# Softmax denominators placed by block transposes and transfers, the mean's tiles read back in exchanged blocks, deeper loads and fewer early mask pieces in a four-layer graph network

## The chip, the cores and the metric

The kernel runs on one core of one Trainium2 chip. The metric is device time in microseconds (us) of one execution; the figure before the change is the median of three runs. The profile is one further execution, recorded by the hardware profiler. TensorE is written PE in profile lines (PEld is its weight load), VectorE DVE, ScalarE ACT, GpSimd POOL and SyncE SP; SP computes nothing and issues transfers (DMAs).

## The reference

A graph network of four layers over 3327 nodes with 512 features and an integer adjacency matrix `adj` of 3327 x 3327. Every layer is followed by a residual and a layer norm. Cut to what matters:

```python
Wh = einsum('ni,hio->hno', h, W)                      # L0: 8 heads of 64
e = leaky_relu(f1[:, :, None] + f2[:, None, :], 0.2)
attention = softmax(where(adj[None] > 0, e, -9e15), axis=-1)
h_prime = einsum('hnm,hmo->hno', attention, Wh)       # L2: the same, then elu
...
keep = (A > 0) & (cumsum(A > 0, axis=1) <= 64)        # L1: first 64 neighbours
nb_mean = keep @ X / maximum(cnt, 1)
xj = leaky_relu(nb_mean @ W_nb.T + b_nb)
xi = leaky_relu(X @ W_line.T + b_line)
return xi + where(cnt > 0, xj, 0)
...
x = layernorm(x + layer(x, adj, ...))                 # L0, L1, L2, L3 in turn
```

L3 is attention as in L2, with 4 heads of 128. Numbers are float32.

## The kernel before

**Tiling.** Nodes are padded to 3328, which is 26 tiles (`NT`) of 128; two halves of 13 tiles (`HALF`, 1664 receiving nodes, `IW`). The transposed adjacency is loaded once as int32 pieces of 128 x 832 (`mask_load`, L547) and turned into an fp8 mask in SBUF (`mask_set`: VectorE L558, or ACT L557). There are 104 pieces: `EARLY` = 82 are handled during L0's projection, the other 22 one per sender tile in the first units of L0's attention, 13 of them on VectorE and 9 on ACT.

**Projection** of a tile: four PE transposes of x (L253), an ACT copy to xT (L255), a reduce (L256), then the matmuls pw (L264), small columns rc, dc and qc on ACT (L265, L268), and VectorE's products vt (L270), which are stored as v. `columns` and `prepare` compute from rc and qc what attention needs for each node (L297 to L315).

**Attention** (`unit`, L357) runs in 8 units for each layer, 2 halves by 4 slots s of 128 features: two heads in a unit for L0 and L2 (`HS` = 2), one for L3. A unit loops over 26 sender tiles j. VectorE makes t from the broadcast row rb, the column qc and the mask (L398, 128 x 1664), ACT makes from t an fp8 step y (L401), PE accumulates po from vj and t in four column cuts (L421) and the denominators pd from y, the mask and pieces of the weights (L373). Then po is copied to ob (ACT L441; in L3's first half VectorE block transposes, L439, and four block transfers to hd, L461), transposed back by PE (pt, L449), copied (hb, L453) and stored to hd by SP (L454). These later steps stand in a list of jobs, one taken for each j of the next unit.

**Denominators.** pd holds for each receiving node partial sums of two kinds in 32-row groups. After a half's last slot (in L3's second half after s=1, 2 and 3) pd is copied to db (ACT L474 and L475, the latter by VectorE in L3), 13 PE matmuls of db with a constant matrix (`sums`, L487) add the parts and put nodes on partitions, and VectorE combines and inverts them (`reciprocals`, L500 to L503). They are the third and fifth job of the next unit, or run directly at a layer's end.

**Finish** (`finish_steps`, L165): for each pair of tiles load h from hd (L126), load xr, divide by the denominators (rec, L180), add or elu (L185 to L194), layer norm (L151 to L161). h and xr have their own buffers.

**sage()** (L610) is layer 1. Stage a: xT (L647, L649), matmuls pz and pi (L655, L658), three bf16 terms of pz, of which one goes to DRAM (zd). Stage b, the mean: for each of 26 tiles 26 x 3 matmuls into acc (L767), with the mask kt made two tiles ahead (PE prefix pk L735, VectorE L739, carries loaded by POOL and copied by ACT L727). `output` (L743) makes the tile's y, normalises it and stores it to x2. The tile's projection for L2 follows as two jobs: `job1` (`project1`) at t = 11 and `job2` (`project2`) at t = 17 of the next tile.

**third()** (L794) normalises L2's output in pairs of tiles and projects them for L3. The loads and steps of one pair are begun before the pair in front of it is projected.

**What sets the order.** PE runs in the order of the program text. On the other engines a scheduler orders the instructions, except where `keep_in_program_order` pins one to its place. Each engine works strictly in its order: an instruction that waits holds up all behind it. SP's transfers, too, are issued in order.

## Time and profile before

| | us |
|---|---|
| median of 3 runs | 3428.16 (3425.46 to 3432.74) |
| profiled execution | 3434.45 |
| its span | 3432.3 |
| PE busy | 3295.2 (96%) |
| VectorE busy | 2666.0 (78%) |
| ACT busy | 2374.3 (69%) |
| mean granted clock of PE | 0.982 |

The span from start to end, by the groups of instructions: L0 projection 0 to 150, L0 attention to 963, sage stage a to 1160, mean 1183 to 1765, L2 attention 1800 to 2572, third 2592 to 2725, L3 attention to 3327 and its tail to 3432; the gaps are changes of stage.

How to read it: "busy" is time in which an engine executes; register, semaphore and transfer-issuing instructions are not counted. A row of instructions has line, engine, operation, output<-input tiles, shapes and count, then busy us and mean ns of one, then the idle time just before it and what ended that. A timeline row has start, length, engine, line, operation and count (neighbouring equal instructions are one row), and in brackets the idle time before it with its releaser. Matmul counts are those of the profile, in which a float32 matmul appears twice.

### The profile page before, as it was taken

The page shows a single profiled execution, that of the slowest core. Times are in us where ns is not written, and L with a number is a line of the kernel's source. Part 1 is how long each engine was busy: PE and PEld are TensorE (multiplying, and loading weights), DVE is VectorE, ACT ScalarE, POOL GpSimd, SP SyncE. Part 2 cuts the span into 40 slices and gives each one's busy share as a digit, 9 for nine tenths or more (in the row PEclk, how much of TensorE's full clock was granted, in tenths as well). Part 3 has the DMA queues.
Part 4 walks back from the last instruction along what each step waited for, and adds up shares of the span by engine and source line. Part 5 has one row for each costly group of instructions (what it writes and reads, how often), then busy time and mean ns, then how long its engine had stood idle before and what let it go on. Part 6 is the DMA issues. An engine that isn't in the chain of part 4 may idle for free.

```text
span 3432.3 us, 47383 instructions
## 1 busy us (share of the span) xinstructions
PE 3295.2 (96%) x18705; PEld 1656.3 (48%) x18705; DVE 2666.0 (78%) x2571; ACT 2374.3 (69%) x2172; POOL 215.1 (6%) x344
## 2 busy tenths in 40 slices
PE   8799999999999899999989999999998999999997
PEld 7544344444444355555543444444446654455553
DVE  5799999999967443434349999999997766668876
ACT  2388999999943233333338999899997655559985
POOL 3200000000010111111110000000001000000000
PEclk9999999999999999999999999999998999999998
DMA  9732111111043422222220111111116411112211
GB/s 372 279 110 69 51 48 43 53 45 39 26 140 125 127 81 76 71 71 73 70 70 25 43 49 48 53 49 46 32 34 219 160 40 40 42 47 89 82 37 48
DMA packets 225061, 276.62 MB, mean 81 GB/s; under 512 B 45949, under 2 KB 160327, under 8 KB 224840
## 3 DMA queue, kind: packets, MB, share of 16 engines
q1 hardware_dynamic: 192280, 162.21, 14.8%
q0 software_dynamic: 27040, 103.70, 9.6%
q10 hardware_dynamic: 5520, 7.69, 0.7%
q8 instruction: 148, 2.42, 0.3%
q14 instruction: 73, 0.60, 0.1%
HBM read 204.92 MB, written 68.60 MB: 80 GB/s over the span
## 4 chain that ended last, share of the span: by engine, by line
PE 73%; issue 12%; DMA 6%; DVE 4%; ACT 3%; POOL 1%; SPq 0%; POOLq 0%; ACTq 0%; DVEq 0%
PE po L421 49%; PE pd L373 7%; PE acc L767 5%; DVE t L398 3%; PE pw L264 3%; PE pz L655 3%; PE pi L658 3%; DMA raw<-in_adjT_dram 2%; DMA cy<-ctd 2%; ACT y L401 1%; PE pt L449 1%; PE pe L487 1%; DMA r<-rr 0%; POOL cy L624 0%; PE pa L966 0%
## 5 line engine op out<-in xcount | busy, mean ns | idle before, releaser
L398 DVE SCALAR_TENSOR_TENSOR t<-rb,qc,mask 128x1664 f32<-128x1664 f32 x1040 | 1959.0, 1945 | 183.1 <-PE po L421 163.6
L401 ACT ACTIVATE y<-t,bi,sc 128x1664 fp8e4<-128x1664 f32 x1040 | 1770.0, 1766 | 321.7 <-PE pd L373 302.9
L421 PE MATMUL po<-t,vj 128*64 128x448 f32 (+3 forms) x8320 | 1912.8, 521 | 24.4 <-DVE t L398 24.2
L421 PEld LDWEIGHTS po<-t,vj 128*64 128x64 f32 (+1 forms) x8320 | 835.0, 148 | 978.1 <-issue 710.6
L767 PE MATMUL acc<-zs,kt 128*128 128x512 bf16 x1352 | 404.7, 381 | 0.0
L767 PEld LDWEIGHTS <-kt 128*128 128x128 fp8e4 x2028 | 199.3, 98 | 246.0 <-issue 9.6
L264 PE MATMUL pw<-wsb,xT 128*128 128x264 f32 (+1 forms) x1248 | 302.7, 398 | 9.6 <-DVE vt L270 5.1
L727 ACT CAST pk<-cy 128x512 f32<-128x512 bf16 x169 | 98.4, 587 | 287.1 <-DVE kt L739 234.0
L264 PEld LDWEIGHTS pw<-wsb,xT 128*128 128x128 f32 x1248 | 241.5, 197 | 55.9 <-ACT xT L255 6.0
L373 PE MATMUL pd<-y,sden 128*32 128x448 fp8e4 (+1 forms) x4160 | 259.4, 342 | 8.2 <-ACT y L401 8.2
L767 PE MATMUL acc<-zl,kt 128*128 128x512 bf16 x676 | 257.5, 381 | 4.6 <-DMA zl<-zd 4.6
L739 DVE SCALAR_TENSOR_TENSOR kt<-pk,mask 128x512 fp8e4<-128x512 f32 x169 | 116.2, 688 | 108.2 <-PE pk L735 107.8
L373 PEld LDWEIGHTS <-sden 128*32 128x32 bf16 x4160 | 117.5, 96 | 160.3 <-issue 137.6
L270 DVE TENSOR_TENSOR vt<-pw,dc 128x256 f32<-128x256 f32 x156 | 59.2, 416 | 136.7 <-ACT dc L265 129.7
L352 POOL DMA_DIRECT2D rb<-r x40 | 21.3, 533 | 1607.9 <-DVE t L398 1593.4
L268 ACT COPY rc<-pw 128x8 f32<-128x8 f32 (+1 forms) x78 | 12.7, 163 | 151.0 <-PE pw L264 151.0
L655 PE MATMUL pz<-wn,xT 128*128 128x512 f32 x208 | 93.7, 593 | 1.2 <-ACT xT L649 1.2
L658 PE MATMUL pi<-wl,xT 128*128 128x512 f32 x208 | 93.5, 592 | 0.0
L558 DVE TENSOR_SCALAR mask<-raw 128x832 fp8e4<-128x832 int32 (+2 forms) x95 | 56.2, 600 | 45.6 <-DMA raw<-in_adjT_dram 45.2
L747 DVE SCALAR_TENSOR_TENSOR y<-acc,cnt,bnb 128x512 f32<-128x512 f32 x26 | 19.5, 751 | 88.5 <-PE acc L767 88.5
L624 POOL DMA_DIRECT2D cy<-ctd x91 | 67.9, 746 | 289.5 <-ACT pk L727 264.8
L256 DVE TENSOR_REDUCE xsum<-xT 128x4 f32<-128x512 f32 x78 | 53.0, 681 | 39.7 <-ACT xT L255 39.3
(175 smaller groups left out, 1738.4 us busy)
## 6 DMA issues: line engine op xcount, KB each, us to landing
vj<-v SPq DMA_DIRECT2D x312, 128.0 KB
rb<-r POOLq DMA_DIRECT2D x40, 832.0 KB, 4.6
raw<-in_adjT_dram SPq DMA_DIRECT2D x67, 416.0 KB
cy<-ctd POOLq DMA_DIRECT2D x78, 256.0 KB, 3.9
h<-hd SPq DMA_DIRECT2D x61, 256.0 KB
v<-vt SPq DMA_DIRECT2D x50, 256.0 KB
hd<-hb SPq DMA_DIRECT2D x48, 256.0 KB
xr<-x POOLq DMA_DIRECT2D x45, 256.0 KB, 3.1
```

What stands on the lines that cost most here:

```text
L264: nc.tensor.matmul(pw[e][:, :FW + H], xT[:, c, :], wsb[:, c, e, :], start=c == 0, stop=c == FC - 1)
L270: nc.vector.tensor_tensor(vt[:, hs, :], pw[e][:, :FW].rearrange("p (h d) -> p h d", d=D), self.dc[:, t, hs].rearrange("p (h e) -> p h e", e=1)
L373: nc.tensor.matmul(pd[c][32 * kk:32 * kk + 32, :w_], lhsT, rhs, start=(kk, c) not in seen, skip_group_check=final is not None, stop=last a ...
L398: nc.vector.scalar_tensor_tensor(t, rb[k], self.qc[:, j, h:h + 1], mask[:, j, i0:i0 + IW], op0=ALU.max, op1=ALU.mult)
L401: nc.scalar.activation(y, t, AF.Sigmoid, bias=self.bi[:, j, h:h + 1], scale=self.sc[:, j, h:h + 1], saturate=False)
L421: nc.tensor.matmul(po[c][k * D:(k + 1) * D, :z - a_], vj[:, j % 2, k * D:(k + 1) * D], ts[k][:, a_:z], start=j == 0, stop=j == NT - 1)
L624: nc.gpsimd.dma_start(out=cy[:, :n, :], in_=ctd[t:t + n, b * GW:(b + 1) * GW] .rearrange("(o t) i -> o t i", o=1).to_broadcast([P, n, GW]))
L655: nc.tensor.matmul(pz, xT[:, c, :], wn[:, c, :], start=c == 0, stop=c == FC - 1)
L658: nc.tensor.matmul(pi, xT[:, c, :], wl[:, c, :], start=c == 0, stop=c == FC - 1)
L727: nc.scalar.copy(pks[k % 2], carry[b, t // 4 * 4][:, t % 4:t % 4 + 2, :])
L739: nc.vector.scalar_tensor_tensor(kt, pk, NEIGHBOURS, mask[:, t:t + 2, i0:i0 + GW], op0=ALU.is_le, op1=ALU.mult, saturate=False)
L767: nc.tensor.matmul(acc, kts[t][:, s * P:(s + 1) * P], zs(t, c) if c < 2 else zl[:, t, :], start=t == 0 and c == 0, stop=t == NT - 1 and c ...
```

## The change

It has four parts. In all but the last of the denominator steps, `sums` and the db copies give way to VectorE's 32 x 32 block transposes of pd, two reduces over the three elements of each sum, four small transfers to a DRAM buffer dd and one transfer back as pes, with nodes on partitions; `finish_sums` then does what `reciprocals` did, as the seventh job of the next unit, at the end of a layer as the last job (in L3's s=2 after five empty jobs). In the mean, tiles 0 to 24 are read back from x2 by four transfers with 32 x 32 blocks exchanged, so that a block transpose on VectorE, pinned in the program's order, gives xT; `job1` comes at t = 17 of the next tile and `job2` at t = 11 of the one after. In third() loads are begun three pairs ahead, with 10 h and 6 xr buffers, the first pairs' h on POOL. `EARLY` is 68, so that 36 pieces fall into attention: 22 on VectorE, 14 on ACT.

In the order built, SP has 100 issues for yx and 35 for dd and pes more than before; on PE 25 x 4 transposes and 7 x 13 matmuls are gone. At half time of L0 and L2 `finish_sums` begins nine tiles of t behind the reduces, in L3 8, 3 and 3.

```diff
@@ -162,7 +162,7 @@
-    def finish_steps(pool, xin, layer, t0, n, hbufs=6, eng=nc.sync):
+    def finish_steps(pool, xin, layer, t0, n, hbufs=6, eng=nc.sync, xbufs=None):
         H, D = layer.H, layer.D
         ys, xs, steps = [], [], []
@@ -171,7 +171,7 @@
                 h = pool.tile([P, F], F32, name="h", bufs=hbufs)
                 load_tile(h, hd, t, eng)
                 ys.append(h)
-                xr = pool.tile([P, F], F32, name="xr")
+                xr = pool.tile([P, F], F32, name="xr", bufs=xbufs)
                 load_tile(xr, xin, t, nc.gpsimd)
                 xs.append(xr)
@@ -247,12 +247,16 @@
             nc.gpsimd.memset(self.sm, 0.0)
-        def project1(self, pool, ps, xt, t):
-            pt = ps.tile([P, FC, P], F32, name="pt")
-            for c in range(FC):
-                nc.tensor.transpose(pt[:, c, :], xt[:, c * P:(c + 1) * P], ident)
+        def project1(self, pool, ps, xt, t, blocks=False):
             xT = pool.tile([P, FC, P], F32, name="xT")
-            nc.scalar.copy(xT, pt)
+            if blocks:
+
+                tc.keep_in_program_order(nc.vector.transpose(xT, xt))
+            else:
+                pt = ps.tile([P, FC, P], F32, name="pt")
+                for c in range(FC):
+                    nc.tensor.transpose(pt[:, c, :], xt[:, c * P:(c + 1) * P], ident)
+                nc.scalar.copy(xT, pt)
             nc.vector.tensor_reduce(xsum[:, :, t], xT, AX.X, ALU.add)
             return xT
@@ -467,48 +471,79 @@
             if s < NS - 1 and not (final and s > 0):
                 return jobs
+
+            ss = slice(0, NS) if not final else slice(0, 2) if s == 1 else slice(s, s + 1)
+            hs = slice(ss.start * HS, ss.stop * HS)
+            r_ = rec[:, t0:t0 + HALF, :H].rearrange("p t (s k) -> p t k s", k=HS)
+            rc = self.rc[:, t0:t0 + HALF, :].rearrange("p t (s k) -> p t k s", k=HS)
             db = sp.tile([P, WA], F32, name="db", bufs=1)
             if WB < WA:
                 nc.gpsimd.memset(db[64:, WB:], 0.0)
+            if not (final and s == NS - 1):
+
+
+                for c in range(2):
+                    nc.vector.transpose(db[:64, c * (WA // 2):(c + 1) * (WA // 2)], pd[c][:64, :WA // 2])
+                    nc.vector.transpose(db[64:, c * (WB // 2):(c + 1) * (WB // 2)], pd[c][64:, :WB // 2])
+                red = sp.tile([P, WA // 32, 2, NS], F32, name="red", bufs=1)
+                dv = db.rearrange("p (b s x) -> p b s x", s=NS, x=8)
+                for o in range(2):
+                    nc.vector.tensor_reduce(red[:, :, o, :], dv[:, :, :, 3 * o:3 * o + 3], AX.X, ALU.add)
+                dd = dram.tile([IW, 2, 2 * NS], F32, name=f"dd{self.li}{half}{s}")
+                for kk in range(4):
+                    i_, w_ = (0, WA) if kk < 2 else (WA, WB)
+                    nc.sync.dma_start(out=dd[i_:i_ + w_, kk % 2, :].rearrange("(b i) x -> i b x", i=32),
+                                      in_=red[32 * kk:32 * kk + 32, :w_ // 32].rearrange("p b o s -> p b (o s)"))
+                pes = sp.tile([P, HALF, 2, 2, NS], F32, name="pes", tag="red", bufs=1)
+                nc.sync.dma_start(out=pes.rearrange("p q k o s -> p q (k o s)"),
+                                  in_=dd.rearrange("(q p) k x -> p q (k x)", p=P))
+
+                def finish_sums():
+                    if HS == 1:
+
+                        tc.keep_in_program_order(
+                            nc.vector.tensor_tensor(pes[:, :, 0], pes[:, :, 0], pes[:, :, 1], op=ALU.add))
+                    for k in range(HS):
+                        ins = nc.vector.scalar_tensor_tensor(r_[:, :, k, ss], pes[:, :, k, 0, ss], 2.0, rc[:, :, k, ss],
+                                                             op0=ALU.mult, op1=ALU.mult)
+                        if HS > 1:
+                            tc.keep_in_program_order(ins)
+                        nc.vector.scalar_tensor_tensor(r_[:, :, k, ss], pes[:, :, k, 1, ss], -2.0, r_[:, :, k, ss],
+                                                       op0=ALU.mult, op1=ALU.add)
+                    nc.vector.reciprocal(rec[:, t0:t0 + HALF, hs], rec[:, t0:t0 + HALF, hs])
+
+                jobs += [nothing] * max(0, 6 - len(jobs))
+                at = 6 if half == 0 or s < NS - 1 else len(jobs)
+                if final and s > 1:
+
+                    return [nothing] * 5 + [finish_sums] + jobs[2:]
+                return jobs[:at] + [finish_sums] + jobs[at:]
+
             for c in range(2):
                 nc.scalar.copy(db[:64, c * (WA // 2):(c + 1) * (WA // 2)], pd[c][:64, :WA // 2])
-                (nc.scalar.copy if HS == 2 else nc.vector.tensor_copy)(
-                    db[64:, c * (WB // 2):(c + 1) * (WB // 2)], pd[c][64:, :WB // 2])
+                nc.vector.tensor_copy(db[64:, c * (WB // 2):(c + 1) * (WB // 2)], pd[c][64:, :WB // 2])
             held = []
             def sums():
-                pe = po[0][:, :2 * HALF * H].rearrange("p (q o h) -> p q o h", q=HALF, o=2) if final and s == NS - 1 else \
-                    qp.tile([P, HALF, 2, H], F32, name="pe", tag="q")
+                pe = po[0][:, :2 * HALF * H].rearrange("p (q o h) -> p q o h", q=HALF, o=2)
                 held.append(pe)
                 for q in range(HALF):
                     e = int(q >= NA)
-                    cc = c1[:, :, 8 * e:8 * e + 8] if HS == 2 else c1w[:, :, e, :]
-                    nc.tensor.matmul(pe[:, q, :, :], db[:, (q - e * NA) * P:(q - e * NA + 1) * P], cc,
+                    nc.tensor.matmul(pe[:, q, :, :], db[:, (q - e * NA) * P:(q - e * NA + 1) * P], c1w[:, :, e, :],
                                      start=True, stop=True)
-
             def reciprocals():
                 pe = held[0]
-
-                ss = slice(0, NS) if not final else slice(0, 2) if s == 1 else slice(s, s + 1)
-                r_ = rec[:, t0:t0 + HALF, :H].rearrange("p t (s k) -> p t k s", k=HS)
-                rc = self.rc[:, t0:t0 + HALF, :].rearrange("p t (s k) -> p t k s", k=HS)
-                pv = pe.rearrange("p t o (k s) -> p t o k s", k=HS)
-                for k in range(HS):
-                    tc.keep_in_program_order(
-                        nc.vector.tensor_tensor(r_[:, :, k, ss], pv[:, :, 0, k, ss], rc[:, :, k, ss], op=ALU.mult))
-                    nc.vector.tensor_tensor(r_[:, :, k, ss], pv[:, :, 1, k, ss], r_[:, :, k, ss], op=ALU.add)
-                hs = slice(ss.start * HS, ss.stop * HS)
+                nc.vector.tensor_tensor(r_[:, :, 0, ss], pe[:, :, 0, ss], rc[:, :, 0, ss], op=ALU.mult)
+                nc.vector.tensor_tensor(r_[:, :, 0, ss], pe[:, :, 1, ss], r_[:, :, 0, ss], op=ALU.add)
                 nc.vector.reciprocal(rec[:, t0:t0 + HALF, hs], rec[:, t0:t0 + HALF, hs])
-            if final and s == NS - 1:
-
-                take = []
-                return [lambda: take.append(transposed(*QUADS[0])), lambda: take.append(transposed(*QUADS[1])),
-                        sums, reciprocals] + [lambda q=q: take[q]() for q in range(2)] + \
-                    [lambda q=q: transposed(*q)() for q in QUADS[2:]]
-            return jobs[:2] + [sums, nothing, reciprocals] + jobs[2:]
+
+            take = []
+            return [lambda: take.append(transposed(*QUADS[0])), lambda: take.append(transposed(*QUADS[1])),
+                    sums, reciprocals] + [lambda q=q: take[q]() for q in range(2)] + \
+                [lambda q=q: transposed(*q)() for q in QUADS[2:]]
@@ -749,7 +784,14 @@
                     nc.vector.scalar_tensor_tensor(y, y, cnt[:, 2, t:t + 1], xi, op0=ALU.mult, op1=ALU.add)
                     norm_rows(sp, [y], t)
                     store_tile(dst, y, t, nc.sync)
-                    return y
+                    if t == NT - 1:
+                        return y
+
+                    yx = sp.tile([P, FC, P], F32, name="yx")
+                    for q in range(4):
+                        nc.sync.dma_start(out=yx[32 * q:32 * q + 32].rearrange("p c (g f) -> p c g f", g=4),
+                                          in_=dst[t * P:(t + 1) * P, :].rearrange("(g a) (c q f) -> q a c g f", g=4, q=4, f=32)[q])
+                    return yx
                 carry_in(0)
                 kts = kept(0, 0) + kept(0, 2)
@@ -771,13 +813,13 @@
                                              len(ahead) < min(NT, t + 10) and t % 2 == 1):
                                 ahead += kept(b + 1, len(ahead))
-                            if jobs and (t == 11 or t == 17 and not (last and s == G - 1)):
+                            if jobs and (t == 11 and t0 + s > 1 or t == 17):
                                 jobs.pop(0)()
                         y = output(acc, t0 + s)
                         held = {}
                         def job1(y=y, t=t0 + s, held=held):
-                            held["xT"] = nxt.project1(sp, ps, y, t)
+                            held["xT"] = nxt.project1(sp, ps, y, t, t < NT - 1)
                         def job2(t=t0 + s, held=held):
                             nxt.project2(sp, bank, wsb, held["xT"], t)
@@ -807,11 +849,25 @@
                 def bank(e):
                     return ps.tile([P, 512], F32, name=f"pw{e}")
+
                 pend = None
                 ahead = first
+                groups = []
+
+                def load_group(t0):
+                    if t0 < NT:
+                        groups.append(finish_steps(fp, x2, L2, t0, 2, 10, nc.gpsimd if t0 < 4 else nc.sync, 6))
+                        groups[-1][1].pop(0)()
+
+                for t0 in (2, 4):
+                    load_group(t0)
                 for t0 in range(0, NT, 2):
-                    ys, ahead = ahead, finish(fp, x2, L2, t0 + 2, 2, 6, nc.sync if t0 else nc.gpsimd) \
-                        if t0 + 2 < NT else None
+                    ys = ahead
+                    load_group(t0 + 6)
+                    if groups:
+                        ahead, steps = groups.pop(0)
+                        for f in steps:
+                            f()
                     for s, y in enumerate(ys):
                         t = t0 + s
                         store_tile(x3, y, t, nc.sync)
@@ -945,7 +1001,7 @@
                 nc.gpsimd.memset(mask[:, NT - 1, :], 0.0)
             nc.gpsimd.memset(mask[:, :, N:NP], 0.0)
             pieces = [(t, q) for t in range(NT) for q in range(2)] + [(t, q) for q in (2, 3) for t in range(NT)]
-            EARLY = 3 * NT + 4
+            EARLY = 5 * NT // 2 + 3
             msteps = mask_steps(rw0, pieces[:EARLY], 5, (), False, 8)
             def load(t):
```

## The prediction

> **What bounds the kernel now.** I read the busy digits first, then the busy time of each engine stage by stage, since the bound changes with the stage. Columns: stretch and its length, then busy time (instructions) of PE, PEld, DVE, ACT and POOL, granted clock, DMA share, GB/s.
>
> ```profile
> 150.00:963.00 813.00, 790.40 (x5819) 338.41 (x5819) 804.26 (x490) 742.41 (x500) 12.13 (x24) 0.99 0.18 54
> 963.00:1160.00 197.00, 192.20 (x543) 94.39 (x544) 130.49 (x248) 69.56 (x120) 14.69 (x27) 0.97 0.38 125
> 1183.00:1765.00 582.00, 569.96 (x2658) 296.50 (x2656) 228.05 (x421) 205.66 (x364) 78.87 (x113) 0.99 0.26 77
> 1800.00:2572.00 772.00, 764.35 (x5458) 344.81 (x5456) 768.97 (x436) 720.13 (x478) 9.62 (x16) 0.99 0.13 41
> 2592.00:2725.00 133.00, 118.63 (x556) 98.78 (x557) 99.88 (x239) 97.64 (x203) 11.82 (x22) 0.95 0.59 193
> 2725.00:3327.00 602.00, 599.07 (x2524) 304.75 (x2522) 429.36 (x349) 412.71 (x294) 17.08 (x30) 1.00 0.21 58
> ```
>
> These are attention of L0, sage stage a, the mean (stage b), attention of L2, third(), attention of L3. In L0 and L2 VectorE is busy 99% and sets the pace; TensorE, at 97%, follows it. In the mean and in L3 TensorE is the bound and VectorE has 60% and 29% free. So VectorE work added in L0 and L2 costs its full time, added in the mean or L3 nothing; TensorE work saved counts only in the mean and L3, and at the starts of stages, where the chain goes from engine to engine.
>
> **Fewer mask pieces first.** 14 pieces (82 to 68) leave the L0 projection. The last 14 mask sets on VectorE there stand at 131.75 to 149.2, mixed with the value products (L270), and wait for their loads; the first t of attention starts at 149.69. Without them the last L270 follow ACT's dc (143.1), and L311 to L315 (1.5 us) end near 145.1: -4.5 (-3.5 if something else there is late, -5 at best). In attention 22 instead of 13 pieces fall to VectorE, 14 instead of 9 to ACT. Nine sets at 0.59 us (L558, 587 ns here) on a full VectorE: +5.3; the five on ACT (0.97 us each) lie in its 9% of room. Sum +0.8.
>
> **Denominators.** Removed: seven of eight groups of 13 matmuls (L487), and ACT's db copies. Added on VectorE for each: four block transposes, two reduces; on SP five small transfers. Rows for the prices:
>
> ```profile
> L256 DVE TENSOR_REDUCE xsum<-xT 128x4 f32<-128x512 f32 x78 | 53.0, 681 | 39.7 <-ACT xT L255 39.3
> ...
> L439 DVE STREAM_TRANSPOSE ob<-po 128x448 f32<-128x448 f32 x8 | 4.7, 625 | 0.0
> ...
> L439 DVE STREAM_TRANSPOSE ob<-po 128x384 f32<-128x384 f32 x8 | 4.0, 541 | 0.0
> ```
>
> Transposes 2 x 0.62 + 2 x 0.54 = 2.3 (64 lanes take as long as 128: the 64x384 copy took 0.557). A reduce of 336 elements a lane lies between the 256-element product's 0.416 and 0.681: 0.5, two are 1.0. The four scalings and the reciprocal cost what they did (4 x 0.21 + 0.80). In L0 and L2 at half time this lands on the bound: 3.3, less the 0.44 that VectorE idles there now (577.58): +2.9 each, **+5.8**. TensorE's 3 us saved there buy nothing. Lower end +2, if ACT's freed 2 us help; upper +9, if the results come late (below).
>
> In L3 TensorE is the bound, and three groups go (half time, s=1, s=2; the last one stays). One displaces 2.82:
>
> ```profile
> 3063.80 2.96 PE L487 MATMUL pe<-c1w,db 128*128 128x8 f32 x26
> 3066.62 4.74 PE L421 MATMUL po<-t,vj 128*128 128x448 f32 x8
> ```
>
> 3 x 2.82 = **-8.5** (-6 to -9.5). VectorE's new work is covered by its room; its finishing step stands behind 3 to 8 tiles of t, 8.7 to 23 us, and three t buffers (8.7 us of PE) cover a stall.
>
> The round trip is the unknown: four transfers in 32-byte rows (3328), then one in 64-byte rows (1664), which SP issues only when the four have landed. Nearest row: L3's block transfers hd<-ob, 128-byte rows, four issues, 6656 packets. DMA busy share in 40 slices of 0.55 us:
>
> ```profile
> DMA  0000016299999479999951000000053000000000
> ...
> hd<-ob SPq DMA_DIRECT2D x4, 208.0 KB
> ```
>
> From 2811.4 fifteen slices, 8.3 us: 1.25 ns a row. A 256 KB load (xi, 2.9 us to landing; 0.7 of it bytes at the 365 GB/s that L0's projection reaches) leaves 2.2 us fixed. By rows: 4.15 + 2.2, then 2.1 + 2.2 = 10.6 us. By bytes (106 KB each, at that row's 100 GB/s): 2 x (1.1 + 2.2) = 6.6 us. I take 10.6: that row is the nearest, and it moves small pieces. At half time nine tiles of t (16.8 us at 1.86) hide it. At the two layer ends nothing does. End of L0:
>
> ```profile
> 962.91 0.84 PE L487 MATMUL pe<-c,db 128*128 128x16 f32 x6 [1.97 <-ACT db L475]
> 965.48 4.45 PE L487 MATMUL pe<-c,db 128*128 128x16 f32 x20 [1.72 <-ACT db L475]
> ...
> 972.97 1.75 PE L647 MATMUL pt<-ident,h 128*128 128x128 f32 x8
> ...
> 984.85 0.66 PE L647 MATMUL pt<-ident,h 128*128 128x128 f32 x4 [1.84 <-ACT h L161]
> ```
>
> Without the sums tile 0's transposes (972.97) come about 7 us earlier. But tile 2's (984.85) need its norm, which on VectorE stands behind the first scaling, and that now waits for pes. pd ends at 960.9; transposes and reduces to 964.7; 10.6 more is 975.5; 7.6 of VectorE (scalings, L180, L194, L152 of tiles 2 to 4 in the order built) and 1.2 of ACT follow: 984.3. So the 7 us turn into idle before tile 2: **-1** (by bytes -4.5, and -8.5 if nothing waited). End of L2, alike: tile 0's transposes move from 2592.09 to about 2586.5 (tile 2's h is now loaded behind the weights on POOL, and L180 for it stands before tile 0's rs on VectorE), but pes lands near 2592, tile 2's transposes near 2598.8 against 2600.58, with the clock cold again after that idle: **-1** (-6 to +2).
>
> **Mean: read-back in place of transposes.** 25 of 26 tiles lose four PE transposes and an ACT copy; VectorE gets a 128x512 transpose (0.7, covered). Price on the bound, from the last matmul before to the next after:
>
> ```profile
> 1511.70 0.38 PE L767 MATMUL acc<-zl,kt 128*128 128x512 bf16 x1
> 1512.93 0.66 PE L253 MATMUL pt<-ident,y 128*128 128x128 f32 x4 [0.85 <-ACT y L161]
> 1513.43 0.59 PE L767 MATMUL acc<-zs,kt 128*128 128x512 bf16 x2
> ```
>
> Matmuls start 0.216 apart, so this gap costs 1.5; untroubled ones cost 0.44. Over the 25: **-16.5** (-11 if the waits for y only move elsewhere).
>
> The transpose is pinned on VectorE and waits for y's store and four read-backs; queued behind it are the next tile's y chain and kt. y's chain takes 9.2 us from the last acc (1503.70 to the store at 1512.90). Read-back X: store 2.9, 2048 rows at 1.25 ns 2.6, landing 2.2: near 8. Chain and read-back form a loop of 9.2 + X against the tile's 22.3 (22.98 measured, less 0.67): X may be 13. The Trainium skill ("VectorE: DVE Perf Modes", section "The three transpose paths") warns here: a plain DMA whose access pattern does the transposing is 19 times slower than the hardware's own path when the innermost stride is large. By that, 0.7 us of bytes become 13 (an estimate), X about 18, and the mean loses 25 x 5. The row stands against it: hd<-ob also exchanges blocks, keeps 128 bytes together, and moves 832 KB in 8.3 us, 3.6 times slower than 365 GB/s, not 19. I go by the row.
>
> **Deeper loads in third().** TensorE waits for ACT's h (L161) at 2627.39, 2646.81 and twice later: 9.7 us, plus 1.4 of cold clock (5.02 for 3.67). Under them VectorE waits 5.2 for xr and 5.7 for h. Loads three pairs ahead end these waits, not the table loads (1.28 each) in the same chain: **-6** (-3 to -10).
>
> **Sum.** 0.8 + 5.8 - 8.5 - 1 - 1 - 16.5 - 6 = -26.4. The profiled execution took 3434.45 (span 3432.3, 2.15 around it); it becomes 3408. It lies 6.3 above the median of 3428.16; I take the difference off the median: **3402**.
>
> **Rivals.** (1) The round trip is short or hidden: the ends give -8.5 and -6.7, third -9, the rest as above: -42, 3387. For it: packets themselves are short. Against: two fixed costs in series at each end. (2) VectorE pays more: finishing steps wait in L0 and L2 (+9), the ends give 0 and +2, the mean only -11, third -3: 0.8 + 9 + 2 - 11 - 3 - 8.5 = -11, 3417. For it: SP issues transfers in order behind vj loads. (3) Slower than before: the read-back loop takes over. It decides from X = 13, and eats the whole change at 13 + 26.4/25 = 14.1; at the skill's 18 the time is 3402 + 125 = 3527. Only the row against it makes it unlikely. (4) The change does nothing: the built order shows the matmuls and transposes gone, so no.
>
> **Chances.** Forecast 0.52, (1) 0.28, (2) 0.17, (3) 0.03, (4) 0. The forecast's unknowns reach from 3391 to 3411; the range 3380 to 3417 takes in (1) and most of (2). A measurement tells 0.2% (6.9 us) from no change: faster 0.92, same 0.05 (the far part of (2), the near part of (3)), slower 0.03.
>
> **What would show it.** Right: mean stage near 566; units of L0 and L2 at half time near 100 instead of 97.7; L3 shorter by 8; VectorE's scaling waiting for pes at both layer ends, and TensorE idle before tile 2. Wrong: no wait for pes there (then the ends give 15), the pinned transpose waiting so long that the acc matmuls stall, or idle before kt.

## The result and the profile after

| | before | after |
|---|---|---|
| median, us | 3429.25 (3425.46 to 3432.74, 4 runs) | 3408.52 (3406.53 to 3410.87, 4 runs) |
| ratio | | 0.994 (0.9923 to 0.9957) |
| profiled execution | 3434.45 | 3407.9 |
| its span | 3432.3 | 3406.2 |

I cut both spans at the same events: the first t of L0's attention, the last pd of L0, the first pk of the mean, the first t and last pd of L2, the first po of L3, the end. Stage lengths in us, with some experiments beside them:

| kernel | to first t | L0 attention | sage a | mean | L2 | third | L3 | span |
|---|---|---|---|---|---|---|---|---|
| before | 149.69 | 811.25 | 206.17 | 620.34 | 788.25 | 147.08 | 709.52 | 3432.3 |
| after | 142.95 | 817.71 | 211.35 | 600.76 | 789.98 | 143.18 | 700.27 | 3406.2 |
| difference | -6.7 | +6.5 | +5.2 | -19.6 | +1.7 | -3.9 | -9.3 | -26.1 |
| late_pt | 141.88 | 818.80 | 212.27 | 612.00 | 789.96 | 144.31 | 699.58 | 3418.8 |
| mid_pe | 141.44 | 814.68 | 209.69 | 603.76 | 786.56 | 140.09 | 701.08 | 3397.3 |
| early82 | 146.09 | 815.29 | 211.08 | 600.88 | 789.99 | 141.89 | 699.18 | 3404.4 |
| l3_pe | 141.49 | 817.82 | 210.59 | 603.58 | 790.02 | 140.76 | 713.04 | 3417.3 |
| best_b | 142.42 | 814.76 | 206.73 | 603.39 | 786.62 | 139.20 | 698.78 | 3391.9 |

These are profiled executions. By the medians the change saves 20.7 us: the profiled execution of before was itself 5.2 above its median (3434.45 for 3429.25), which flatters the -26.1.

Where the code of a stage is the same, it differs between the runs by 0.1 us in L2 (apart from yx3, 0.5, and yx2, 2.1), 1.3 in L0's attention, 2.5 in L3, 3.2 at the start and in sage a, and 4.3 in third; a difference is read against that.

Busy time by stretch of after (columns as in the table before):

```profile
143.00:961.00 818.00, 794.99 (x5796) 344.29 (x5797) 812.48 (x504) 743.83 (x498) 10.37 (x19) 0.99 0.20 61
1183.00:1754.00 571.00, 562.94 (x2585) 288.21 (x2584) 243.42 (x447) 191.34 (x339) 79.64 (x114) 0.99 0.35 93
2563.00:2706.00 143.00, 117.22 (x563) 98.39 (x561) 111.85 (x268) 102.67 (x208) 17.68 (x33) 0.92 0.65 215
2706.00:3307.00 601.00, 598.07 (x2476) 300.36 (x2475) 438.52 (x368) 411.08 (x294) 17.28 (x31) 1.00 0.22 59
```

The bounds are the old ones: VectorE fills L0 (99%), TensorE the mean and L3 (99%). What is new is the DMA share of the mean, 0.35 for 0.26; third() is still the stretch of these with most room on TensorE (82% busy).

**Half time of L0** answers to the unit where TensorE had 26 matmuls pe. VectorE, then SP:

```profile
568.42 0.64 DVE L486 STREAM_TRANSPOSE db<-pd 64x448 f32<-64x448 f32 x1
569.08 0.59 DVE L487 STREAM_TRANSPOSE db<-pd 64x384 f32<-64x384 f32 x1
...
572.82 0.98 DVE L491 TENSOR_REDUCE red<-db 128x112 f32<-128x336 f32 x2
...
590.48 0.21 DVE L507 SCALAR_TENSOR_TENSOR rec<-pes,rc 128x52 f32<-128x52 f32 x1
```

```profile
573.83 2.08 SPq L495 DMA_DIRECT2D dd<-red  x4
...
577.66 0.38 SPq L498 DMA_DIRECT2D pes<-dd  x1
```

The transposes, 2 x (0.64 + 0.59), and the reduces, 0.98, cost 3.4; the prediction had 3.3. SP needs 4.2 us from the first issue to the last, and pes is used 12.8 us after it was issued, without a wait. From its first t to that of the next unit the unit took 101.54 us, for 98.62 before: 2.9 more. In L2 it took 101.37 for 99.67, only 1.7 more, because before lost time there in another way: around its matmuls pe TensorE was granted a clock of 0.83, and VectorE was busy for 18.47 of 20 us, where after had 1.00 and 20.00 (before first, then after; the clock is the third number from the right):

```profile
2190.00:2210.00 20.00, 20.00 (x128) 9.87 (x126) 18.47 (x16) 15.33 (x10) 0.20 (x1) 0.83 0.05 14
2190.00:2210.00 20.00, 19.96 (x140) 9.09 (x136) 20.00 (x17) 18.63 (x14) 0.00 (x0) 1.00 0.14 40
```

**End of L0.** SP, VectorE, TensorE and ACT of after, one block each:

```profile
962.18 0.98 SPq L458 DMA_DIRECT2D hd<-hb  x2
964.19 10.69 SPq L495 DMA_DIRECT2D dd<-red  x4
974.98 1.02 SPq L458 DMA_DIRECT2D hd<-hb  x2
977.25 0.36 SPq L498 DMA_DIRECT2D pes<-dd  x1
```

```profile
963.21 0.96 DVE L491 TENSOR_REDUCE red<-db 128x112 f32<-128x336 f32 x2
979.80 0.22 DVE L507 SCALAR_TENSOR_TENSOR rec<-pes,rc 128x52 f32<-128x52 f32 x1 [15.63 <-DMA pes<-dd]
```

```profile
964.19 1.36 PE L682 MATMUL pt<-ident,h 128*128 128x128 f32 x8 [1.17 <-ACT h L161]
975.61 6.38 PE L690 MATMUL pz<-wn,xT 128*128 128x512 f32 x8 [10.06 <-ACT xT L684]
981.83 3.60 PE L693 MATMUL pi<-wl,xT 128*128 128x512 f32 x8
988.31 1.11 PE L682 MATMUL pt<-ident,h 128*128 128x128 f32 x4 [2.89 <-ACT h L161]
```

```profile
974.30 0.77 ACT L457 COPY hb<-pt 128x512 f32<-128x512 f32 x2 [9.45 <-DMA hd<-hb]
974.98 1.07 ACT L684 COPY xT<-pt 128x512 f32<-128x512 f32 x2
```

ACT and SP of before at the same place:

```profile
974.42 0.90 ACT L453 COPY hb<-pt 128x512 f32<-128x512 f32 x2 [1.78 <-DMA hd<-hb]
975.23 1.07 ACT L649 COPY xT<-pt 128x512 f32<-128x512 f32 x2
```

```profile
971.50 3.89 SPq L454 DMA_DIRECT2D hd<-hb  x3
```

The same four issues that took 2.08 us at half time take 10.69 here. VectorE waits 15.63 for pes. A second wait was not foreseen. hb has two buffers. Without the sums in front of them, its first two stores are issued at 962.18 instead of from 971.50, ahead of dd in SP's order, but into the traffic of the stage's loads. The third copy into hb waits 9.45 for the first of these stores, until 974.30, 12.1 us after its issue; in before that copy comes at 974.42, 2.9 us after the store's issue. Behind the copy stands xT, for which TensorE idles 10.06, so that tile 0's pz starts at 975.61, no earlier than in before (975.87). Tile 0's transposes come 3.5 us after pd's end (before: 12.0), but tile 2's 27.7 us after it (before: 23.9).

**Mean.** Where TensorE had four transposes (pt) for each tile, after has none for tiles 0 to 24. VectorE, from kt to the next y, and SP's issues for the same tile:

```profile
1440.08 0.69 DVE L774 SCALAR_TENSOR_TENSOR kt<-pk,mask 128x512 fp8e4<-128x512 f32 x1 [0.42 <-PE pk L770]
1441.33 0.71 DVE L254 STREAM_TRANSPOSE xT<-yx 128x512 f32<-128x512 f32 x1 [0.56 <-DMA yx<-x]
1442.08 0.69 DVE L260 TENSOR_REDUCE xsum<-xT 128x4 f32<-128x512 f32 x1
1446.56 0.75 DVE L782 SCALAR_TENSOR_TENSOR y<-acc,cnt,bnb 128x512 f32<-128x512 f32 x1 [3.79 <-PE acc L809]
```

```profile
1433.81 0.33 SPq L133 DMA_DIRECT2D x<-y  x1
1436.92 2.61 SPq L792 DMA_DIRECT2D yx<-x  x4
```

From the store of y to the transpose pass 7.5 us, of which VectorE waits 0.56; all its waits for yx in the mean are 11.4 us in 11 cases, none over 1.8, and in these 11 tiles the way from store to transpose takes 7.5 to 9.1 us. In most others it is 10.3, without a wait for yx: there VectorE's order, not the read-back, sets the time of the transpose. VectorE then still waits 3.79 for acc: TensorE stays the bound. Tiles follow each other after 22.12 and 21.47 us in turn, where it was 22.9 and 21.9.

**L3, half time.** The row that answers to pe between po and po is a row without a gap:

```profile
3039.70 10.21 PE L425 MATMUL po<-t,vj 128*128 128x448 f32 x29
```

**third().** TensorE's waits for h in the whole stage (total, times, longest), from 2575.7 to 2723 in before and from 2562.7 to 2706 in after, and then the rows in after where they fall at its start:

```profile
PE pt L253 <- ACT h L161: 13.6, 5, 3.9
```

```profile
PE pt L258 <- ACT h L161: 10.6, 3, 8.8
```

```profile
2575.44 1.97 PE L258 MATMUL pt<-ident,h 128*128 128x128 f32 x8 [10.61 <-DMA xr<-x]
2577.28 4.34 PE L268 MATMUL pw<-wsb,xT 128*128 128x260 f32 x16
2590.47 1.12 PE L258 MATMUL pt<-ident,h 128*128 128x128 f32 x4 [8.85 <-ACT h L161]
```

The wait of 10.61 for tile 0 is put down to xr; tile 0 still comes 12.7 after pd's end, for 16.4 in before. In before 3.9 of the 13.6 is the wait for tile 0 (2592.09), and tile 2 (2600.58) doesn't wait at all; the other four waits make 9.7. Of these later waits 1.7 is left in after. But tile 2 now waits 8.85, so that the stage is only 3.9 shorter.

### The profile page after: what moved, and what is told of

The parts are those of the page before. It is cut to its first block, busy times and chain, and to the rows that moved or that the text cites. A ratio compares the mean times of both kernels' runs of the same rounds, so it can differ in the third digit from the quotient of the medians.

```text
span 3406.2 us, 47019 instructions
## 1 busy us (share of the span) xinstructions
PE 3262.8 (96%) x18423; PEld 1631.0 (48%) x18423; DVE 2695.3 (79%) x2630; ACT 2351.4 (69%) x2128; POOL 214.7 (6%) x344
## 4 chain that ended last, share of the span: by engine, by line
PE 79%; issue 7%; DVE 6%; DMA 4%; ACT 2%; POOL 0%; SPq 0%; ACTq 0%; POOLq 0%; DVEq 0%
PE po L425 49%; PE acc L809 9%; PE pd L377 7%; PE pw L268 5%; DVE t L402 4%; PE pz L690 3%; PE pi L693 3%; DMA raw<-in_adjT_dram 2%; ACT y L405 1%; PE pt L453 1%; DMA cy<-ctd 1%; PE pk L770 1%; PE pt L258 0%; PE pa L1022 0%; DVE mask L593 0%
## 5 line engine op out<-in xcount | busy, mean ns | idle before, releaser
L425 PE MATMUL po<-t,vj 128*64 128x448 f32 (+3 forms) x8320 | 1924.6, 520 | 25.0 <-DVE t L402 22.3
L425 PEld LDWEIGHTS po<-t,vj 128*64 128x64 f32 (+1 forms) x8320 | 848.3, 148 | 978.2 <-issue 689.7
L356 POOL DMA_DIRECT2D rb<-r x40 | 21.9, 548 | 1617.0 <-DVE t L402 1604.5
L272 ACT COPY rc<-pw 128x8 f32<-128x8 f32 (+1 forms) x78 | 12.7, 163 | 138.7 <-PE pw L268 136.2
L782 DVE SCALAR_TENSOR_TENSOR y<-acc,cnt,bnb 128x512 f32<-128x512 f32 x26 | 19.5, 751 | 85.9 <-PE acc L809 85.9
```

Source lines behind the costliest of these rows:

```text
L425: nc.tensor.matmul(po[c][k * D:(k + 1) * D, :z - a_], vj[:, j % 2, k * D:(k + 1) * D], ts[k][:, a_:z], start=j == 0, stop=j == NT - 1)
```

## The experiments

The theory: the parts act as the prediction has them, and at the layer ends the round trip is lengthened by loads that share the transfers. The rivals: the round trip is slow by itself, from its short rows, whatever runs beside it; the mean gained only from the later place of the jobs, not from the transposes; and the read-back is near the length at which its loop would slow the mean. Each kernel changes the kernel after in one place, unless said otherwise. The kernel before was timed again beside them: 3431.66 us beside ends_pe, no_wl, late_pt and one_pair, 3432.43 beside mid_pe, early82, ramp2 and best_a2, 3431.24 beside the rest.

**ends_pe** and **mid_pe**: the denominators of L0 and L2 by TensorE again, in the first at the layers' ends, in the second at half time. **l3_pe**: the same for L3's three groups.

```diff
-            if not (final and s == NS - 1):
+            if not (final and s == NS - 1) and not (HS == 2 and half == 1):   # ends_pe
+            if not (final and s == NS - 1) and not (HS == 2 and half == 0):   # mid_pe
+            if not (final and s == NS - 1) and not (HS == 1):                 # l3_pe
```

(The db copies, `sums` with c1, `reciprocals` and `return jobs[:2] + [sums, nothing, reciprocals] + jobs[2:]` of before are put back for these.)

> The changed kernel, but the denominators at the ends of L0 and L2 are summed by TensorE again, as before the change; the half-time and L3 denominators stay with VectorE and the transfers. Theory (the dd and pes round trip sits on the path at the two layer ends, because its small rows share the DMA engines with the next stage's loads, and SP's stores and ACT's copies queue behind it): from the end of L0's pd to the first pk of the mean 206 us again instead of 211.4 (-5.2), from the end of L2's pd to L3's first po 139 to 141 instead of 143.3 (-2 to -4): about 3401 us. Rival (the time at the ends is lost to the shifted loads, masks or clock, not to the round trip): both stretches stay within 1 us of the changed kernel's, about 3408 us.

> The changed kernel, but at half time of L0 and L2 the denominators are summed by TensorE again, as before the change; layer ends and L3 stay with VectorE and the transfers. Theory (VectorE sets the pace there, so its 3.4 us of transposes and reduces cost about their time): L0's attention takes 814.7 us instead of 817.7, L2's 788.3 instead of 790.0, in all 4 to 5 us less, ratio to before 0.9926. Rival (TensorE's saved matmuls and ACT's saved copies pay for it): no difference of more than 1 us in either.

> The changed kernel, but L3's denominators are summed by TensorE again, as before the change; L0 and L2 stay with VectorE and the transfers. Theory (TensorE is the bound in L3 and three groups of 13 matmuls displace 2.8 us each): from L3's first po to the end 708.5 to 710 us instead of 700.3, about 8.5 to 9 us slower than the changed kernel, ratio to before 0.996 to 0.997. Rival (VectorE's new steps and the pes wait in L3 cost what the matmuls save): within 2 us of 700.3.

ends_pe: 3406.59, ratio 0.9924 (0.9909 to 0.9939). Sage a is 207.01 for 211.35, so transposing at L0's end loses 4.3 us. The other profiles bear it out: the four kernels with TensorE's sums there (before, ends_pe, best_a2, best_b) have 206.2 to 207.0, the nine with the round trip and wl's load 209.1 to 212.3. At L2's end TensorE's sums gain nothing: tile 2 comes 29.4 after pd's end, 27.7 in after, so that the theory came true at the first end only. mid_pe: 3401.15, 0.9908 (0.9893 to 0.9923); L0's attention is 3.0 and L2 3.4 shorter than in after, the price of VectorE's work on its own bound. l3_pe: 3419.22, 0.9966 (0.9953 to 0.9979); L3 is 12.8 longer than in after. Its half time:

```profile
3039.69 5.75 PE L425 MATMUL po<-t,vj 128*128 128x448 f32 x16
3045.28 3.34 PE L536 MATMUL pe<-c1w,db 128*128 128x8 f32 x26
3048.47 5.89 PE L425 MATMUL po<-t,vj 128*128 128x448 f32 x8
```

Three times 3.19 (3045.28 to 3048.47) is 9.6. The other 3.2 us lie in the clock: in this stretch l3_pe was granted 0.83 and after 1.00, which over 20 us is 3.4 (an estimate from these two rows, l3_pe first). l3_pe's L3 is also 3.5 longer than before's (709.52).

```profile
3036.00:3056.00 20.00, 20.00 (x92) 11.58 (x93) 12.44 (x13) 8.26 (x7) 0.20 (x1) 0.83 0.37 63
3036.00:3056.00 20.00, 20.00 (x85) 10.37 (x84) 17.67 (x17) 10.43 (x6) 0.20 (x1) 1.00 0.44 68
```

**no_wl**: the 1 MB load of wl at L0's end is left out and pi uses wn (so pi is computed from the wrong weights).

```diff
-                wl = load_w(wp, wlT, "wl", nc.gpsimd)
+                wl = wn
```

> The changed kernel without the 1 MB load of wl: pi is computed with wn instead, so xi has the wrong weights; nothing else is left out. Theory (contention with the stage's loads stretches the dd transfers at the end of L0): SP's four dd issues there take 3 to 8 us instead of 10.7, and pes is there 13 us or less after the reduces instead of 15.6. Rival (32-byte rows cost the same wherever they run): dd issues stay at 10 to 11 us and VectorE's wait at 15 to 16 us.

3401.7 in one run. SP and VectorE:

```profile
965.72 5.85 SPq L495 DMA_DIRECT2D dd<-red  x4
```

```profile
975.69 0.69 DVE L180 TENSOR_TENSOR h<-h,rec 128x512 f32<-128x512 f32 x1 [5.34 <-DMA h<-hd]
976.86 0.21 DVE L507 SCALAR_TENSOR_TENSOR rec<-pes,rc 128x52 f32<-128x52 f32 x1 [0.48 <-DMA pes<-dd]
```

The issues take 5.85 for 10.69, and from the first of them to that of pes pass 8.5 us (965.72 to 974.23) for 13.1; at half time it was 3.8. So wl's load makes up about half of what the round trip loses here; the stage's other loads stayed, and what they cost alone wasn't tried. Tile 2 comes 20.0 after pd's end for 27.7, but not all of that is the load's price. pes is used 11.1 us after dd's first issue for 15.6, which is 4.5. The other 3.2 come from VectorE's order, which is another one in this kernel: three steps L180 stand in front of the first scaling with pes instead of behind it, and from that scaling to tile 2's transposes it takes 5.3 us for 8.5. The wait for pes itself (0.48) is short because VectorE waits 5.34 for an h just before it.

**one_pair** (third()'s loop as before) and **ramp2** (only one pair is loaded ahead of the loop, and ahead of the weights wsb; the next follow later, and from the fifth tile on the loads are as deep as in after):

```diff
-                    ys = ahead
-                    load_group(t0 + 6)
...
+                    ys, ahead = ahead, finish(fp, x2, L2, t0 + 2, 2, 6, nc.sync if t0 else nc.gpsimd) \
+                        if t0 + 2 < NT else None
```

```diff
-                for t0 in (2, 4):
-                    load_group(t0)
+                due = list(range(2, NT, 2))
+                load_group(due.pop(0))
+                wsb = wp.tile([P, FC, 2, FW + L3.H], F32, name="wsb")
...
-                    load_group(t0 + 6)
+                    while due and due[0] <= (2, 6)[t0 // 2] if t0 < 4 else due and due[0] <= t0 + 6:
+                        load_group(due.pop(0))
```

> The changed kernel with third() loading one pair ahead as before the change. Theory (deeper loads remove the later waits for ACT's h, 6 to 7 us, while the start is ruled by the round trip of the denominators): from the end of L2's pd to L3's first po 149 to 151 us instead of 143.3, TensorE waiting for ACT h some 9 us more after tile 4: about 3415 us. Rival (the deeper loads themselves crowd the dd transfers at the start, and give back what they gain): the four dd issues fall from 8.1 to under 5 us, and the stretch stays within 2 us of 143.3.

> The changed kernel with the loads of third() growing from one pair ahead at its start to three pairs ahead from the fifth tile on, and the first pair's loads issued before the weights'. Theory (the deeper loads gain later and cost at the start, where they and the weights come before tile 2's h and share the DMA engines with dd): tile 2's transposes come 22 to 24 us after L2's last pd instead of 27.7, four dd issues under 7 us, and from there to L3's first po 136 to 140 us instead of 143.2. Rival (the later waits do not depend on depth, so the start is only moved): 142 to 144 us.

one_pair: 3413.28, 0.9946 (0.9932 to 0.9961); third 143.59. Its SP issues:

```profile
2571.22 4.40 SPq L495 DMA_DIRECT2D dd<-red  x4
```

against, in after:

```profile
2568.35 8.12 SPq L495 DMA_DIRECT2D dd<-red  x4
```

and VectorE's wait for pes is 0.27 for 5.85. I split third() at tile 2's transposes:

| us | pd's end to tile 2 | tile 2 to L3 |
|---|---|---|
| before | 24.9 | 122.2 |
| one_pair | 22.8 | 120.8 |
| after's third(), eight kernels | 27.1 to 28.2 | 112.5 to 116.6 |
| ends_pe (after's third(), sums on TensorE) | 29.4 | 114.1 |
| best_b (ramp2's third(), sums on TensorE) | 26.8 | 112.4 |

So the rival came true: the deeper loads gain 4 to 8 us once the stage runs and lose 4.3 to 5.4 at its start. The loss is there with TensorE's sums too (29.4 in ends_pe for 24.9 in before, 4.5), so it isn't the round trip alone: with either way of summing, tile 2 comes later when more is loaded ahead. In one_pair TensorE's later waits for h are as short as in after (2.0 from 2592 to 2725), but 5.2 for vt and 5.2 for rr stand in their place, in after 2.2 and 1.6; why was not tried. ramp2: 3403.52, 0.9916 (0.9901 to 0.9931), third 140.33; dd's issues take 10.13 and tile 2 comes at 27.2. The start wasn't cured, against the theory, and the gain isn't beyond the 4.3 by which this stage scatters.

**late_pt**: no read-back, TensorE transposes as before, but the jobs at after's later places.

```diff
-                    yx = sp.tile([P, FC, P], F32, name="yx")
...
-                    return yx
+                    return y
...
-                            held["xT"] = nxt.project1(sp, ps, y, t, t < NT - 1)
+                            held["xT"] = nxt.project1(sp, ps, y, t)
```

> The changed kernel with the new places of the two projection jobs in the mean (t = 17, and t = 11 of the tile after) but with TensorE's four transposes and ACT's copy in place of the read-back. Theory (11 us of the mean's gain are TensorE time, the rest, 6 to 9 us, are waits for y that the later place alone removes): the stretch from the first pk to L2's first t takes 611 to 613 us against 600.8 with the read-back and 620.4 before: about 3419 us. Rival (the later place is what gains): the stretch stays under 604 us, about 3409 us. Second rival (the whole gain is the transposes'): 619 to 621 us, about 3427 us.

3417.45, 0.996 (0.9946 to 0.9975). The mean takes 612.00: of its 19.6 us, 8.3 come from the later places alone (before to late_pt) and 11.2 from the transposes, 0.45 for each of 25 tiles. In late_pt the transposes stand between other matmuls without a wait for y:

```profile
1446.59 0.38 PE L802 MATMUL acc<-zl,kt 128*128 128x512 bf16 x1
1446.81 0.60 PE L258 MATMUL pt<-ident,y 128*128 128x128 f32 x4
1447.24 0.59 PE L802 MATMUL acc<-zs,kt 128*128 128x512 bf16 x2
```

In before such waits make 2.4 us in seven tiles (1205 to 1755), and 2.0 of the 8.3 lie behind the last tile; where the rest lies is open.

**early82**: `EARLY = 3 * NT + 4`, as before.

> The changed kernel with 82 mask pieces in L0's projection again, as before the change. Theory by the profiles (14 pieces fewer bring the first t forward by 6.8 us, and the pieces moved to attention cost 3.6 us there): first t at 149 to 150 us instead of 143, L0's attention 814 us instead of 817.7, about 3 us slower in all. Rival, the prediction's own sum (-4.5 and +5.3): 0.8 us faster in all.

3406.75, 0.9926 (0.9911 to 0.9941). The first t is 1.5 to 4.7 later than in the three kernels beside it, L0's attention 2.4 shorter than in after: nothing in sum that these runs can tell from zero.

**yx2**, **yx3**: the four read-backs twice and three times over, `for q in [0, 1, 2, 3] * 2` and `* 3`. This tests the rival whose loop was to decide from X = 13.

> The changed kernel, but every read-back of the mean is made twice, one after the other into the same tile. Theory (chain of y and read-back form a loop of 9 + X, X is 8 us in the changed kernel and one more pass costs 4 to 5, so the loop takes 21 to 22 us against a tile's 21.8): the stretch from the first pk to L2's first t takes 601 to 612 us instead of 600.8. Rival (the read-back is no loop, VectorE's room hides any length): 601 us here and also with three passes. Second rival (any lengthening is paid at once): 25 x 4.5, over 700 us.

> The changed kernel, but every read-back of the mean is made three times, one after the other into the same tile. Theory (loop of 9 + X with X near 17, so 26 against a tile's 21.8): tiles about 4 us apart more than in the changed kernel, the stretch from the first pk to L2's first t 690 to 720 us, about 3510 us in all. Rival (no loop): 601 to 605 us.

One run each: 3421.74 and 3423.62; the mean takes 615.35 and 617.40. VectorE and SP of yx3:

```profile
1404.26 0.75 DVE L782 SCALAR_TENSOR_TENSOR y<-acc,cnt,bnb 128x512 f32<-128x512 f32 x1 [5.78 <-PE acc L809]
...
1411.38 0.69 DVE L774 SCALAR_TENSOR_TENSOR kt<-pk,mask 128x512 fp8e4<-128x512 f32 x1 [1.38 <-PE pk L770]
1411.99 0.70 DVE L254 STREAM_TRANSPOSE xT<-yx 128x512 f32<-128x512 f32 x1
```

```profile
1391.00 0.33 SPq L133 DMA_DIRECT2D x<-y  x1
1393.54 12.58 SPq L792 DMA_DIRECT2D yx<-x  x12
```

X, the time from store to transpose, is 21.0 (1391.00 to 1411.99), and the loop formula asks for 30 us a tile. Tiles follow after 21.9 and 22.3, so that neither theory came true. The transpose now stands behind the next tile's y (L782), not ahead of it as in after: the pin doesn't hold y's chain back, and the scheduler took the chain first. In yx2 X is about 16.4, with the same order in 23 of 25 tiles. What the longer read-back costs in yx3 is 0.2 to 0.4 us in most tiles, a wait of 7.0 on the last read-back's transpose at the end of the stage, where after waits 3.9, and a longer tile where L2's preparation falls (33.93 for 26.88). The loop of the prediction exists only in the order of after, and no run has a long X in that order: what it would cost there was not measured.

**best_a2** and **best_b**: ramp2's third(), and TensorE's sums again in L0 and L2; best_a2 keeps the transposes at L2's end (`not (HS == 2 and not (self.li == 2 and half == 1))`), best_b nowhere in L0 and L2 (`not (HS == 2)`).

> The changed kernel with TensorE's sums at half time of L0 and L2 and at the end of L0, the round trip kept at the end of L2 and in L3, and the growing loads of third() of the run before. Theory: L0's attention 814.7 us, end of L0 to the mean 207, L2's attention 788.3, third 136 to 140, the rest as in the changed kernel: 11 to 15 us faster than it, ratio to before about 0.990. Rival (each saving only exposes the next wait): less than 7 us faster than it.

> The changed kernel with TensorE's sums in all of L0 and L2, half time and ends, the round trip only in L3, and the growing loads of third(). Theory (every round trip that stands on a path or on a full VectorE is gone): like the run best_a2 (3397.2 us span) but for the start of third, where the sums stand before the transposes again but no pes is waited for: 3394 to 3399 us. Rival (the end of L2 is better with the round trip): 3400 us or more.

best_a2: 3397.61, 0.99 (0.9884 to 0.9917). best_b: 3394.38, 0.9893 (0.9877 to 0.991), the fastest, its interval clear of after's, though not of best_a2's. It keeps what pays where TensorE is the bound (mean, L3), and gives back 3.0 in L0's attention, 4.6 in sage a and 3.4 in L2. Its mean, like that of the other kernels with TensorE's sums in part, is 2.6 to 4.1 longer than after's. The tile with the preparation takes 28.46 for 26.88, and behind it, from 1480 to 1520, all five were granted a clock of 0.96 and after 1.00, which over 40 us is that 1.6 (an estimate); the rest, and what lowers the clock, was not tried.

## Why the prediction held, step by step

The time forecast was 3402; it came to 3408.52, where before itself took 1.1 more than in the runs shown: by the medians -20.7 for -26.4. That the profiles give -26.1 is luck in part. Errors cancelled, and that execution of before was slow by its start (some 3.6 against early82) and by the low clock in L2 (some 1.5).

- **Mask pieces, +0.8.** In the two profiles -6.7 at the start and about +3.5 in attention. early82, with the pieces of before, starts 3.6 ahead of before and 3.1 behind after, so that about half of the -6.7 is how that run of before started. Right within the scatter.
- **Half time of L0 and L2, 2 x 2.9.** L0 +2.9; L2 +1.7 from before to after, 3.4 by mid_pe, the clock in before making the difference. The units' own times, 98.62 and 99.67 before and 101.5 after, lie above the 97.7 and 100 that were to show it. The prices of the row for a block transpose carried over to 64 lanes, and the cover of nine tiles of t held.
- **L3, -8.5.** -9.3 (-12.8 against l3_pe, of which some 3.4 is clock). Right.
- **End of L0, -1.** It was +5.2, and this step failed: "I take 10.6 us: that row is the nearest". The row, hd<-ob, was read in a quiet stretch. Here the round trip ran beside the 1 MB load of wl and loads of h and xr, SP was held 10.69 us by dd's issues alone, and pes came 15.63 after VectorE was ready. no_wl shows wl's load to be a cause, worth about half of it; the rest is put down to the other loads without a run of their own. In the quiet of half time the same price was too high instead: there 3.8 us pass from dd's first issue to that of pes, for the 6.35 of the sum (4.15 + 2.2). The step also missed a queue: hb's first two stores, now issued into the same loads, hold up ACT's third copy and xT behind it, so that TensorE idled mainly before tile 0's pz (10.06) and not before tile 2 (2.89). That the scaling stands in front of all steps L180 is a matter of the built order: in no_wl it stands behind three of them, which is worth 3.2. At tile 2 the loss is 3.7 (27.7 for 23.9). The other 1.4 lies just behind it: TensorE was granted a clock of 0.83 from 984 to 994 in after and of 1.00 from 981 to 991 in before. mid_pe and ramp2, which had 1.00 there too, don't have the 1.4.
- **End of L2 and third(), -1 and -6.** In sum -3.9 for -7. The parts were +2.8 and -6.7. The second term was right. The first was right for the denominators alone (one_pair: -2.1), and was overturned by the change's own deeper loads, which the working priced only where they gain (tile 2 came 2.8 later, for 1.8 earlier in the sum).
- **Mean, -16.5.** -19.6. X, "near 8", was 7.5 to 9.1 where VectorE waited for it. The transposes give 11.2, as the lower bound of 11 had it. The other 5.5 of the sum stood for waits for y, which were 2.4 in before; the later place of the jobs, which has no term of its own, gives 8.3. So the mechanism was right for 11 of the 16.5.
- **The rival that ends slower.** The rule of the Trainium skill ("VectorE: DVE Perf Modes", "The three transpose paths"), a transfer 19 times slower than the hardware's path when the access pattern does the transposing and the innermost stride of the destination is large, would have made X about 18 by the prediction's estimate; the trace has 7.5 to 9.1 with rows of 128 bytes kept together, whose innermost stride is one element, so that the rule's condition isn't met. And X near 16 in yx2 and from 19 to 23 in yx3 (one run each) cost some 15 us, not the 100 of the loop, since the built order put y's chain first; in after's order the loop stays untested. Rival (1)'s terms add up to -42.6, so 3386 and not 3387.

## What to carry to other kernels

Move work from TensorE to VectorE and transfers stage by stage: it paid where TensorE was the bound (mean, L3) and cost where VectorE was (L0, L2), and the version that does only the first, best_b, is the fastest, with ramp2's loads in third(). Price a round trip through DRAM from a row in the stretch where it will run, with the loads that are issued there, and then ask what else of the chain moves into these loads and what stands behind a copy that waits. A gain that is read from one pair of profiles is also held against the granted clock of both: some 3.4 us in l3_pe and 1.5 in L2 of before were clock. Deeper loads are priced at their start too, where they share the transfers with the work that opens the stage.

## What the hardware showed that was not expected

- Four issues of transfers in 32-byte rows held SP for 2.08 us at L0's half time, 4.40 at L2's end without the deeper loads, 8.12 with them, 5.85 at L0's end without wl's load and 10.69 with it. Issues behind them in the queue waited that long, and a store of hb that was issued 2 us ahead of the 10.69 kept its buffer for 12.1 us.
- Read-backs in 128-byte rows stayed cheap: four in the mean held SP 2.61 us, and between 1205 and 1760 the DMA share rose only from 0.33 to 0.40 and 0.47 with two and three passes.
